# A graph attention kernel: one node span and one bank of sums for eight edge tiles instead of four

## The chip, the cores and the metric

The kernel runs on one core of a Trainium2 chip. The metric is device time in microseconds (us) of the whole program, as the median of several executions. A separate profiled execution of the same program gives the profile. Its engines are called PE (TensorE, matrix products), DVE (VectorE), ACT (ScalarE), POOL (GpSimd, which here issues the gathers) and SP (SyncE, which here issues the other transfers).

## The reference, cut to what matters

The input is a graph of 6250 nodes with 768 features each and 100,000 edges, sorted by their destination node. The layer normalises x, applies two graph attention layers (four heads, then one) and a small network of two dense layers, and adds the result to x:

```python
h = (x @ W).reshape(n, heads, -1)
e = leaky_relu(alpha_s[src] + alpha_d[dst], 0.2)      # one score per edge and head
e = exp(e - segment_max(e, dst)[dst])
alpha = e / (segment_sum(e, dst)[dst] + 1e-16)
out = segment_sum(h[src] * alpha, dst)                # sum over the edges of a node
```

Each node also has an edge to itself. What matters for this case is the last line: for every edge a row of h has to be fetched by its source, weighted, and added to the sum of its destination. As the edges are sorted, consecutive edges belong to the same or to neighbouring nodes; on average a node has 16 edges, so 128 edges cover about 8 nodes.

## The kernel before

**Tiles, groups and spans.** An edge tile is 128 edges, one per partition. There are 784 places for tiles (`NET`), in 196 groups of four (`NG`, `TPG`), or 98 units of two groups (`NU`). Nodes are in 49 tiles of 128 (`NT`). Group g covers 512 edges, some 32 nodes. The kernel pads 256 edges ahead of the first (`LEAD = 2 * P`), so that group g's edges lie around node 32g. It assumes that all their destinations lie in the span of 128 nodes from 32g-64 on. `hold` (L848) computes from `wbase` (L104) whether every edge's destination is in its group's span; if it is not, `general` (L959) recomputes everything in a slower way. As 256 padded edges are two tiles, the first group has two tiles of real edges (`FIRST`), the last has four; `tiles(g)` (L540) says which. There are 782 real tiles.

**Three stages.** A first stage normalises x and computes h for all nodes with TensorE (about the first 145 us), and writes it to a table in memory. Then `layer_edges` (L529) runs once for each attention layer.

**A group in `layer_edges`.** The loop over g (L706) does in order of each engine's queue:
- `gather(g + 8)` (L544): one indirect DMA per tile, issued by POOL, fetches 128 rows of the table into G. Two tiles share a buffer, of which there are 20.
- `pair(g, 0)` and, later in the group, `pair(g, 1)` (L613): for two tiles, ACT takes two exponentials of the source scores (L620, L622), DVE combines them with the factor of the destination (L625, and L635 or L628) to the weight w. In layer 1, DVE multiplies the gathered rows by w (`hw`, L637), and TensorE multiplies the one-hot matrix of destinations (`hot`, L583) by them; in layer 2, DVE makes a one-hot matrix that contains the weights (L632), and TensorE multiplies it by the gathered rows. Either way L648 adds the four tiles of a group into one PSUM bank, `o_ps[g]`. The row of a node in that sum is its number modulo 128, whatever the span. Three banks, under the tag "o", are in use in turn.
- The destination factors of each edge come from a matmul (`meet`, L593) of a mask with `pre.win`, whose entry is chosen by the group's span. The masks are made by DVE in layer 1 (`make_mask`, L561), stored to memory one unit of eight tiles at a time, and fetched again in layer 2 (`fetch_mask`, L523).
- `gather_up(g - 2)` (L659) at the end of a group takes up the bank of two groups earlier: `acc` is the running sum times `keep`, plus the bank (L673). `keep` (L117) is 0 in the one quarter (32 nodes) that enters the span anew, so old sums are dropped there, and 1 elsewhere. The quarter that has just left the span is then complete, and ACT copies it into `sum` (L681). After four quarters a node tile is complete, and its further work is put into the list `late`.
- `advance` (L685), twice a group, and four times in two groups near the end, lets each piece of work in `late` go one step on. In layer 1 (`Node1.steps`, L794) that is dividing, transposing, multiplying by W2 and writing the row block of layer 2's table (L817); in layer 2 (`Node2.steps`, L900) the two dense layers, adding x, and writing the output (L946).

**The ends.** The order of the last groups is written out by hand. Layer 2's first 11 tiles are gathered early (`first_rows`, L292, L300), by GpSimd behind layer 1's last gather: two of them need the table as far as node tile 45, nine as far as node tile 46; rows of later nodes are put in from on-chip copies (`first_whole`, L262). All other gathers of layer 2 need the whole table. For the last node tile, `whole` takes the sum of all groups but the last ahead of time, and only the last group's bank is added at the end.

**What sets the order.** Every engine works through its own queue in the order of the program; there is no planner. DVE's queue has, in one group: pair 0's three or four operations, the next one-hot matrix, the mask, pair 1's operations, and the addition of `gather_up`. Behind that addition stand the next group's pairs. ACT's copy of a quarter waits for the addition, and the next pair's exponentials are behind the copy.

Of the kernel before, what the change touches and what calls it, by code (L numbers as in the profile page):

```python
# [10 lines left out]
F32 = mybir.dt.float32  # L11
# [3 lines left out]
ALU = mybir.AluOpType  # L15
AX = mybir.AxisListType

P = 128
# [9 lines left out]
NT = -(-N // P)  # L28
NQ = 4 * NT
TPG = 4  # L30
NG = NQ
LEAD = 2 * P
EP = NG * TPG * P
NET = NG * TPG
FIRST = LEAD // P
# [18 lines left out]
def kernel(  # L54
# [33 lines left out]
    def bcast(src, n, off=0):  # L88
# [12 lines left out]
    nid = const.tile([P, NT], F32, name="nid")  # L101
    nc.gpsimd.iota(nid, pattern=[[P, NT]], base=0, channel_multiplier=1,
                   allow_small_or_imprecise_dtypes=True)
    wbase = const.tile([P, NG, TPG], F32, name="wbase")  # L104
    nc.gpsimd.iota(wbase, pattern=[[32, NG], [0, TPG]], base=-64, channel_multiplier=0,
                   allow_small_or_imprecise_dtypes=True)

    iota_ps = ps.tile([P, P], F32, name="iota_ps", bufs=1)
# [5 lines left out]
    ones_c = const.tile([P, 1], F32, name="ones_c")  # L114
    nc.vector.memset(ones_c, 1.0)

    keep = const.tile([P, 4], F32, name="keep")  # L117
    nc.vector.memset(keep, 1.0)
    for k in range(4):
        nc.vector.memset(keep[32 * k:32 * k + 32, k:k + 1], 0.0)  # L120

# [399 lines left out]
    def fetch_mask(u):  # L523

        if u < NU:
            mask[u] = maskp.tile([P, 8 * P], BF16, name="mask")
            nc.sync.dma_start(mask[u], mask_d[u * P:(u + 1) * P])

    def layer_edges(layer, H, node, pre, matched, pre_pool):  # L529

# [3 lines left out]
        with tc.tile_pool(name=f"eg{layer}", bufs=4) as eg, \  # L534
# [5 lines left out]
            def tiles(g):  # L540

                return range(max(TPG * g, FIRST) - TPG * g, min(TPG * g + TPG, LAST) - TPG * g)
# [18 lines left out]
            def make_mask(u):  # L561

                if not 0 <= u < NU:
                    return
                if layer == 2:
                    return fetch_mask(u + 1)
                a, b = (t * P for t in both(u))
                mask[u] = maskp.tile([P, 8 * P], BF16, name="mask")
                if u == 0:
                    nc.vector.memset(mask[u][:, :a], 0.0)  # L570
                at = u % 2 * 8 * P
                nc.vector.tensor_scalar(mask[u][:, a:b], drow[u // 2][:, at + a:at + b], pidx, None,  # L572
                                        ALU.is_equal)
                nc.sync.dma_start(mask_d[u * P:(u + 1) * P], mask[u])

            def make_hot(g):

# [15 lines left out]
            def meet(t):  # L593

                if t >= NT:
                    return
                e_ps[t] = ps.tile([P, 16, 6 * H], F32, name="e_ps", tag="e")
                for u, at, a, b in ranges(t):
                    m = mask.pop(u)
                    for k in range(a, b):  # L600
                        nc.tensor.matmul(e_ps[t][:, at + k, :3 * H], m[:, k * P:(k + 1) * P],  # L601
                                         pre.win[:, 2 * u + k // TPG + 1], start=True, stop=True)

            def join(t):
                if t >= NT:
# [7 lines left out]
            def pair(g, p):  # L613

                if 2 * p not in tiles(g):
                    return
                Gp = G.pop(TPG // 2 * g + p)
                sc = Gp[:, :, RW[1]:] if layer == 1 else Gp[:, :, HID:HID + 1]
                e1 = sm.tile([P, 2, H], F32, name="e1")
                nc.scalar.activation(e1, sc, AF.Exp)  # L620
                e2 = sm.tile([P, 2, H], F32, name="e2")
                nc.scalar.activation(e2, sc, AF.Exp, scale=SLOPE)  # L622
                at = TPG * (g % 4) + 2 * p
                rho, v, w = (e_ps[g // 4][:, at:at + 2, k * H:(k + 1) * H] for k in range(3, 6))
                nc.vector.tensor_mul(v, e2, rho)  # L625
                if layer == 2:
                    w = sm.tile([P, 2, H], F32, name="w")
                    nc.vector.tensor_max(w, v, e1)  # L628
                    hw = hwp.tile([P, 2, P], F32, name="hw")
                    for t in range(2):  # L630
                        k = TPG * g + 2 * p + t
                        nc.vector.tensor_scalar(hw[:, t], iota_ps, dcol[:, k:k + 1], w[:, t],  # L632
                                                ALU.is_equal, ALU.mult)
                else:
                    nc.vector.tensor_max(w, v, e1)  # L635
                    hw = hwp.tile([P, 2, H, C + 1], F32, name="hw")
                    nc.vector.tensor_mul(  # L637
                        hw, Gp[:, :, :RW[1]].rearrange("p t (h c) -> p t h c", h=H),
                        w.unsqueeze(3).to_broadcast([P, 2, H, C + 1]))
                if g not in o_ps:  # L640
                    o_ps[g] = ps.tile([P, RW[layer]], F32, name="o_ps", tag="o", bufs=3)
                for t in range(2):
                    k = 2 * p + t
                    if layer == 2:
                        l, r = hw[:, t], Gp[:, t]
                    else:
                        l, r = hot[g][:, k], hw[:, t].rearrange("p h c -> p (h c)")
                    nc.tensor.matmul(o_ps[g], l, r[:, :RW[layer]], start=(k == tiles(g)[0]),  # L648
                                     stop=(k == TPG - 1))

            def stay_warm(n):

# [3 lines left out]

            done, run, late, idle_ps = {}, {}, [], []

            def gather_up(g):  # L659

                if not 0 <= g < NG:
                    return
                last = g == NG - 1
                if last:

                    late.append(node.steps(NT - 1, None, run[0], o_ps.pop(g)))
                    return
                acc = sums.tile([P, RW[layer]], F32, name="acc")
                if g == 0:
                    nc.vector.tensor_copy(acc, o_ps.pop(g))  # L670
                else:
                    k = (g + 1) % 4
                    nc.vector.scalar_tensor_tensor(acc, run[0], keep[:, k:k + 1],  # L673
                                                   o_ps.pop(g), ALU.mult, ALU.add)
                run[0] = node.whole(NT - 1, acc) if g == NG - 2 else acc
                t, q = divmod(g - 2, 4)
                if 0 <= t < NT - 1:
                    if q == 0:
                        done[t] = sums.tile([P, RW[layer]], F32, name="sum", bufs=3)
                    r = slice(32 * q, 32 * q + 32)  # L680
                    nc.scalar.activation(done[t][r], acc[r], AF.Copy)  # L681
                    if q == 3:
                        late.append(node.steps(t, done.pop(t)))

            def advance(g):  # L685

# [19 lines left out]
            for g in range(NG):  # L706
# [4 lines left out]
                pair(g, 0)  # L711
                if g == NG - 1:
                    pair(g, 1)
                if g >= NG - 2:
                    gather_up(g - 1)
                advance(g)
                if g <= NG - 4:
                    make_hot(g + 1)
# [17 lines left out]
                advance(g)  # L736
                if j == 3:
                    join(t + 1)
                if g < NG - 2:
                    gather_up(g - 2)  # L740
                if g == NG - 3:
                    gather_up(g - 1)
                if NG - 3 <= g < NG - 1:
                    stay_warm(3)
                hot.pop(g, None)
                if layer == 1 and g == NG - 6:
                    first_sources(2)
            gather_up(NG - 1)
            advance(NG)
            stay_warm(4)  # L750
            if layer == 1:
# [501 lines left out]
```

## Time and profile before

| | |
|---|---|
| median of 3 executions | 2574.66 us (2572.14 to 2586.72) |
| the profiled execution's own time | 2137.04 us |
| its span, from first to last instruction | 2135.3 us |
| granted TensorE clock, mean over the span | 0.825 |
| PE busy | 1589.5 us (74%) |
| DVE busy | 1416.1 us (66%) |
| ACT busy | 593.1 us (28%) |
| POOL busy | 1600.6 us (75%) |

The profiled execution is 437.6 us faster than the median of the others. In lines of the profile, L12 is line 12 of the kernel, "out<-in" names what an instruction writes and reads, and "xcount" says how often it ran. Of a group of instructions the page gives the busy time and the mean of one in ns, and then, behind a second bar, how long the engine was idle just before them and what ended most of that idle time. "issue" stands where nothing that the profile shows was waited for. DMA-issuing instructions of SP and ACT are not counted as busy; the gathers of POOL are, for the time in which POOL prepares them.

### The profile page before, as it was taken

The page shows a single profiled execution, that of the slowest core. Times are in us where ns is not written, and L with a number is a line of the kernel's source. Part 1 is how long each engine was busy: PE and PEld are TensorE (multiplying, and loading weights), DVE is VectorE, ACT ScalarE, POOL GpSimd, SP SyncE. Part 2 cuts the span into 40 slices and gives each one's busy share as a digit, 9 for nine tenths or more (in the row PEclk, how much of TensorE's full clock was granted, in tenths as well). Part 3 has the DMA queues.
Part 4 walks back from the last instruction along what each step waited for, and adds up shares of the span by engine and source line. Part 5 has one row for each costly group of instructions (what it writes and reads, how often), then busy time and mean ns, then how long its engine had stood idle before and what let it go on. Part 6 is the DMA issues. An engine that isn't in the chain of part 4 may idle for free.

```text
span 2135.3 us, 26701 instructions
## 1 busy us (share of the span) xinstructions
PE 1589.5 (74%) x6763; PEld 1075.4 (50%) x6765; DVE 1416.1 (66%) x4359; ACT 593.1 (28%) x2601; POOL 1600.6 (75%) x1759
## 2 busy tenths in 40 slices
PE   8996777766767677666768677777767777777777
PEld 6874444444444444444445445545545545545544
DVE  7887777667677777677777655555555555555554
ACT  4651222222222222222222222222222222222222
POOL 6877777777777777777777777777777777777774
PEclk9998888677777767887779888888888888888888
DMA  9976666555555565565556455565555555565553
GB/s 356 363 232 206 169 172 176 165 169 163 167 170 163 170 170 162 169 168 158 166 143 211 130 180 166 169 181 166 169 181 166 169 181 166 169 181 167 168 171 114
DMA packets 157544, 383.26 MB, mean 179 GB/s; under 512 B 35543, under 2 KB 49966, under 8 KB 157382
## 3 DMA queue, kind: packets, MB, share of 16 engines
q0 software_dynamic: 75072, 209.10, 36.6%
q1 hardware_dynamic: 80940, 170.88, 23.1%
q10 hardware_dynamic: 1370, 1.48, 0.2%
q8 instruction: 58, 0.95, 0.2%
q14 instruction: 104, 0.85, 0.1%
HBM read 323.13 MB, written 58.19 MB: 179 GB/s over the span
## 4 chain that ended last, share of the span: by engine, by line
DMA 27%; PE 26%; DVE 26%; issue 9%; ACT 7%; POOL 5%; ACTq 0%; SPq 0%; POOLq 0%; DVEq 0%
DMA G<-table,src_i 26%; PE o_ps L648 11%; DVE hw L637 8%; PE y_ps L937 7%; POOL G L553 4%; PE h_ps L350 4%; DVE acc L673 3%; DVE e_ps L625 3%; ACT sum L681 3%; DVE e_ps L635 2%; ACT e L620 2%; DVE hw L632 2%; DVE mask L572 1%; ACT e L622 1%; PE y_ps L873 1%
## 5 line engine op out<-in xcount | busy, mean ns | idle before, releaser
L553 POOL DMA_INDIRECT G<-table,src_i x1545 | 1470.1, 952 | 472.3 <-issue 260.5
L648 PE MATMUL o_ps<-hw,hot 128*128 128x260 f32 x1564 | 596.7, 520 | 282.9 <-DVE hw L637 221.4
L648 PE MATMUL o_ps<-G,hw 128*128 128x258 f32 x1564 | 469.1, 432 | 229.8 <-DVE hw L632 229.1
L648 PEld LDWEIGHTS o_ps<-hw,hot 128*128 128x128 f32 x1564 | 352.9, 248 | 492.9 <-DVE hw L637 359.2
L625 DVE TENSOR_TENSOR e_ps<-e,e_ps 128x8 f32<-128x8 f32 (+1 forms) x782 | 128.4, 164 | 598.9 <-ACT e L622 597.5
L648 PEld LDWEIGHTS o_ps<-G,hw 128*128 128x128 f32 x1564 | 309.9, 212 | 348.3 <-DVE hw L632 290.5
L681 ACT ACTIVATE sum<-acc 32x260 f32<-32x260 f32 (+1 forms) x384 | 159.9, 416 | 776.9 <-DVE acc L673 775.3
L620 ACT ACTIVATE e<-G 128x8 f32<-128x8 f32 (+1 forms) x782 | 159.9, 204 | 617.8 <-DMA G<-table,src_i 576.4
L632 DVE TENSOR_SCALAR hw<-iota_ps,dcol,w 128x128 f32<-128x128 f32 x782 | 285.0, 406 | 14.4
L637 DVE TENSOR_TENSOR hw<-G,e_ps 128x520 f32<-128x520 f32 x391 | 271.9, 695 | 15.2 <-DVE e_ps L635 2.0
L937 PE MATMUL y_ps<-wm,mT 128*128 128x384 f32 x392 | 206.5, 664 | 0.7 <-ACT mT L926 0.7
L673 DVE SCALAR_TENSOR_TENSOR acc<-acc,keep,o_ps 128x260 f32<-128x260 f32 (+1 forms) x388 | 184.5, 476 | 0.1
L622 ACT ACTIVATE e<-G 128x8 f32<-128x8 f32 (+1 forms) x782 | 148.9, 190 | 0.2
L350 PE MATMUL h_ps<-w,r 128*128 128x256 f32 x588 | 133.0, 380 | 4.4 <-ACT r L341 4.4
L583 DVE TENSOR_TENSOR hot<-iota_ps,dcol 128x512 f32<-128x512 f32 (+1 forms) x196 | 133.5, 682 | 0.0
L937 PEld LDWEIGHTS y_ps<-wm,mT 128*128 128x128 f32 x392 | 88.3, 249 | 66.9 <-issue 40.9
L350 PEld LDWEIGHTS h_ps<-w,r 128*128 128x128 f32 x588 | 108.0, 190 | 21.8 <-ACT r L341 5.7
L635 DVE TENSOR_TENSOR e_ps<-e_ps,e 128x8 f32<-128x8 f32 x391 | 68.1, 174 | 13.4
L365 POOL TENSOR_TENSOR ha<-kept,a1b 128x512 f32<-128x512 f32 x45 | 53.2, 1183 | 23.9 <-ACT kept L356 23.8
L628 DVE TENSOR_TENSOR w<-e_ps,e 128x2 f32<-128x2 f32 x391 | 62.2, 159 | 13.3
L601 PEld LDWEIGHTS <-mask 128*128 128x128 bf16 x1564 | 57.7, 101 | 11.4 <-issue 1.7
L767 ACT ACTIVATE rT<-tp,bT 128x128 f32<-128x128 f32 x196 | 59.4, 352 | 6.6 <-PE tp L761 6.4
(405 smaller groups left out, 1137.7 us busy)
## 6 DMA issues: line engine op xcount, KB each, us to landing
xt<-in_x SPq DMA_DIRECT2D x96, 384.0 KB, 4.8
drow<-dmod_d SPq DMA_DIRECT2D x49, 512.0 KB, 6.4
mask_d<-mask SPq DMA_DIRECT2D x98, 256.0 KB, 2.2
mask<-mask_d SPq DMA_DIRECT2D x98, 256.0 KB, 5.9
G<-table,src_i POOLq DMA_INDIRECT x1545, 2.9
xTt<-in_xT SPq DMA_DIRECT2D x49, 384.0 KB, 5.9
out<-y SPq DMA_DIRECT2D x48, 384.0 KB
table<-kept SPq DMA_DIRECT2D x49, 132.0 KB, 3.7
```

The costliest lines, as they stand in the source:

```text
L350: nc.tensor.matmul(h_ps, r[:, k], w1[:, k], start=(k == 0), stop=(k == KI - 1))
L553: nc.gpsimd.indirect_dma_start(out=G[k // 2][:, k % 2], out_offset=None, in_=table[layer], in_offset=bass.IndirectOffsetOnAxis(ap=src_i[:, ...
L583: nc.vector.tensor_tensor(hot[g][:, T[0]:T[0] + n], iota_ps.unsqueeze(1).to_broadcast([P, n, P]), dcol[:, k:k + n].unsqueeze(2).to_broadca ...
L620: nc.scalar.activation(e1, sc, AF.Exp)
L622: nc.scalar.activation(e2, sc, AF.Exp, scale=SLOPE)
L625: nc.vector.tensor_mul(v, e2, rho)
L632: nc.vector.tensor_scalar(hw[:, t], iota_ps, dcol[:, k:k + 1], w[:, t], ALU.is_equal, ALU.mult)
L637: nc.vector.tensor_mul(hw, Gp[:, :, :RW[1]].rearrange("p t (h c) -> p t h c", h=H), w.unsqueeze(3).to_broadcast([P, 2, H, C + 1]))
L648: nc.tensor.matmul(o_ps[g], l, r[:, :RW[layer]], start=(k == tiles(g)[0]), stop=(k == TPG - 1))
L673: nc.vector.scalar_tensor_tensor(acc, run[0], keep[:, k:k + 1], o_ps.pop(g), ALU.mult, ALU.add)
L681: nc.scalar.activation(done[t][r], acc[r], AF.Copy)
L937: nc.tensor.matmul(y_ps, mT[:, j], wm2[:, j, s * half:(s + 1) * half], start=False, stop=(j == KH - 1))
```

## The change

One span of 128 nodes now serves a unit of two groups. The padding ahead of the first edge goes (`LEAD = 0`), so unit u covers 1024 edges around nodes 64u to 64u+63, and its span is the 128 nodes from 64u-32 on. Group 0 has four real tiles then, and the last group two; there are still 782. All eight tiles of a unit use the same entry of `pre.win`, and their products are added up in one bank, `o_ps[u]`. `gather_up(u)` takes it up at the end of group 2u+5 (other groups near the end), and copies two finished quarters at once instead of one; `keep` is 0 in the two quarters that enter the span. In the last but one unit a quarter that is no longer part of the last node tile is cleared. Masks are stored and fetched only as wide as they have real tiles. `wbase`, from which the guard is computed, follows the new spans.

```diff
-LEAD = 2 * P
+LEAD = 0
...
-    wbase = const.tile([P, NG, TPG], F32, name="wbase")
-    nc.gpsimd.iota(wbase, pattern=[[32, NG], [0, TPG]], base=-64, channel_multiplier=0,
+    wbase = const.tile([P, NU, 2 * TPG], F32, name="wbase")
+    nc.gpsimd.iota(wbase, pattern=[[64, NU], [0, 2 * TPG]], base=-32, channel_multiplier=0,
...
-    keep = const.tile([P, 4], F32, name="keep")
+    keep = const.tile([P, 2], F32, name="keep")
     nc.vector.memset(keep, 1.0)
-    for k in range(4):
-        nc.vector.memset(keep[32 * k:32 * k + 32, k:k + 1], 0.0)
+    for k, q in ((0, 1), (0, 2), (1, 3), (1, 0)):
+        nc.vector.memset(keep[32 * q:32 * q + 32, k:k + 1], 0.0)
...
         if u < NU:
+            b = (min(8 * u + 8, LAST) - 8 * u) * P
             mask[u] = maskp.tile([P, 8 * P], BF16, name="mask")
-            nc.sync.dma_start(mask[u], mask_d[u * P:(u + 1) * P])
+            nc.sync.dma_start(mask[u][:, :b], mask_d[u * P:(u + 1) * P, :b])
...
-                if u == 0:
-                    nc.vector.memset(mask[u][:, :a], 0.0)
...
-                nc.sync.dma_start(mask_d[u * P:(u + 1) * P], mask[u])
+                nc.sync.dma_start(mask_d[u * P:(u + 1) * P, a:b], mask[u][:, a:b])
...
-                                         pre.win[:, 2 * u + k // TPG + 1], start=True, stop=True)
+                                         pre.win[:, 2 * u + 2], start=True, stop=True)
...
-                if g not in o_ps:
-                    o_ps[g] = ps.tile([P, RW[layer]], F32, name="o_ps", tag="o", bufs=3)
+                u = g // 2
+                if u not in o_ps:
+                    o_ps[u] = ps.tile([P, RW[layer]], F32, name="o_ps", tag="o", bufs=3)
...
-                    nc.tensor.matmul(o_ps[g], l, r[:, :RW[layer]], start=(k == tiles(g)[0]),
-                                     stop=(k == TPG - 1))
+                    nc.tensor.matmul(o_ps[u], l, r[:, :RW[layer]], start=(g % 2 == 0 and k == 0),
+                                     stop=(g % 2 == 1 and k == tiles(g)[-1]))
...
-            def gather_up(g):
-
-                if not 0 <= g < NG:
-                    return
-                last = g == NG - 1
-                if last:
-
-                    late.append(node.steps(NT - 1, None, run[0], o_ps.pop(g)))
+            def gather_up(u):
+
+                if u == NU - 1:
+
+                    late.append(node.steps(NT - 1, None, run[0], o_ps.pop(u)))
                     return
                 acc = sums.tile([P, RW[layer]], F32, name="acc")
-                if g == 0:
-                    nc.vector.tensor_copy(acc, o_ps.pop(g))
+                if u == 0:
+                    nc.vector.tensor_copy(acc, o_ps.pop(u))
                 else:
-                    k = (g + 1) % 4
-                    nc.vector.scalar_tensor_tensor(acc, run[0], keep[:, k:k + 1],
-                                                   o_ps.pop(g), ALU.mult, ALU.add)
-                run[0] = node.whole(NT - 1, acc) if g == NG - 2 else acc
-                t, q = divmod(g - 2, 4)
-                if 0 <= t < NT - 1:
+                    nc.vector.scalar_tensor_tensor(acc, run[0], keep[:, u % 2:u % 2 + 1],
+                                                   o_ps.pop(u), ALU.mult, ALU.add)
+                for Q in (2 * u - 1, 2 * u):
+                    t, q = divmod(Q, 4)
+                    if not 0 <= t < NT - 1:
+                        continue
...
+                if u == NU - 2:
+                    nc.vector.memset(acc[96:], 0.0)
+                    run[0] = node.whole(NT - 1, acc)
+                else:
+                    run[0] = acc
...
-                if g >= NG - 2:
-                    gather_up(g - 1)
+                if g == NG - 2:
+                    gather_up(NU - 2)
...
-                if g < NG - 2:
-                    gather_up(g - 2)
-                if g == NG - 3:
-                    gather_up(g - 1)
+                if g % 2 and 5 <= g < NG - 6:
+                    gather_up((g - 5) // 2)
+                elif g in (NG - 6, NG - 5, NG - 3):
+                    gather_up({NG - 6: NU - 5, NG - 5: NU - 4, NG - 3: NU - 3}[g])
...
-            gather_up(NG - 1)
+            gather_up(NU - 1)
```

## The prediction, made before the result was known

> **What bounds the kernel now.** I read the page's busy shares first, then equal stretches of both edge passes, then GpSimd's instructions one by one where the passes begin and end, and last the chain of waits inside layer 1. The span of the profiled execution is 2135.3 us, its own time 2137.04 us.
>
> ```profile
> span 2135.3 us, 26701 instructions
> ...
> PE 1589.5 (74%) x6763; PEld 1075.4 (50%) x6765; DVE 1416.1 (66%) x4359; ACT 593.1 (28%) x2601; POOL 1600.6 (75%) x1759
> ```
>
> VectorE (DVE) and GpSimd (POOL) are both well short of full by this count. The costliest groups show what the rest of POOL's time is.
>
> ```profile
> L553 POOL DMA_INDIRECT G<-table,src_i x1545 | 1470.1, 952 | 472.3 <-issue 260.5
> L681 ACT ACTIVATE sum<-acc 32x260 f32<-32x260 f32 (+1 forms) x384 | 159.9, 416 | 776.9 <-DVE acc L673 775.3
> L673 DVE SCALAR_TENSOR_TENSOR acc<-acc,keep,o_ps 128x260 f32<-128x260 f32 (+1 forms) x388 | 184.5, 476 | 0.1
> ```
>
> A gather (L553) keeps POOL for 952 ns, with about 0.30 us before the next: 1545 of them leave 472.3 us of gaps, 0.306 each. The stretches of 400 us (columns PE, PEld, DVE, ACT, POOL) show whether those gaps ever grow:
>
> ```profile
> 200.00:600.00 400.00, 282.55 (x1121) 183.73 (x1121) 297.65 (x828) 97.17 (x495) 303.33 (x318) 0.78 0.60 169
> 600.00:1000.00 400.00, 278.30 (x1077) 181.81 (x1076) 286.28 (x796) 97.47 (x476) 303.12 (x319) 0.76 0.59 166
> 1200.00:1600.00 400.00, 301.18 (x1354) 200.76 (x1354) 229.07 (x825) 108.87 (x499) 302.63 (x320) 0.84 0.57 172
> 1600.00:2000.00 400.00, 305.33 (x1362) 203.98 (x1362) 228.70 (x822) 109.75 (x500) 302.53 (x321) 0.84 0.58 172
> ```
>
> They do not. POOL does 318 to 321 gathers in every stretch, 1.25 us each, although layer 2 asks a fifth less of VectorE and more of TensorE than layer 1. So the gathers set the pace: four tiles, one group, take 5.0 us. GpSimd's order of time where layer 1 hands over to layer 2 shows the only stall:
>
> ```profile
> 1130.08 0.95 POOL L553 DMA_INDIRECT G<-table,src_i  x1 [0.30 <-issue]
> 1131.33 0.95 POOL L300 DMA_INDIRECT G<-table,first_i  x1 [0.30 <-DVE e_ps L625]
> ...
> 1133.82 0.95 POOL L300 DMA_INDIRECT G<-table,first_i  x1 [0.30 <-ACT e L620]
> ...
> 1146.78 0.94 POOL L553 DMA_INDIRECT G<-table,src_i  x1 [1.89 <-DVE G L275]
> ```
>
> Layer 2's early gathers follow layer 1's last without a pause; the one idle of 1.89 us, 1.59 above the usual, comes when the gathers need the whole table. In all, 1564 gathers run from 144.6 to 2111.6 us: 1967 of 2135.3, with 144.6 ahead and 23.7 behind. The compute beside them has slack. This is the chain inside layer 1, at a place where it is catching up:
>
> ```profile
> 601.78 0.43 ACT sum L681
> 602.23 0.21 ACT e L620
> ...
> 605.63 0.41 DVE acc L673
> 606.06 0.42 ACT sum L681
> ```
>
> From one sum to the next is one group: 4.28 us through ScalarE and VectorE, 0.7 under the gathers' 5.0.
>
> **Profiled time and runs.** The median, 2574.66, is 1.2048 times the profiled execution's 2137.04, and the profile does not say why. [...] I take all engines to be slowed alike in the timed runs, so that POOL bounds them too and ratios carry over.
>
> [...]
>
> **The change, part by part** (times of the profiled execution).
>
> *VectorE's take-up.* Before, each layer has 194 additions at L673 and one copy; after, one copy and 96 additions. So 196 fewer in all: 196 x 0.476 = 93.3 us of VectorE. Worth 0, because gathers hide it; were that cover gone it is at most 93.3 us, 4.4%. It widens slack: a group without take-up skips 0.41 (addition) + 0.43 (copy) + 0.32 (the exponentials queued behind the copy) = 1.16 us of the 4.28 chain and comes to 3.1; one with it has a second copy and comes to 4.7. Mean 3.9.
>
> *ScalarE's copies of finished quarters.* 192 a layer before and after; two come together, so the next pair's exponentials wait 0.42 us longer in every second group. Under the same cover: 0.
>
> *Small VectorE work.* Two new memsets on 32 partitions x 260. Not shown; those shown take 0.06 (128x1) and 0.17 us (128x128): 0.06 to 0.5 each, I take 0.2, ahead of layer-end work that waits for later matmuls anyhow. The first mask's memset (0.17) goes. 0, at most 1.
>
> *Bank.* The 3128 matmuls of L648 stay; one bank collects eight. Unit u+3's first matmul needs the bank of u, whose addition stands in VectorE's queue at the end of group 2u+5, ahead of the weights (L637, L632) that this matmul waits for anyway. 0. Exposed each time it would be 96 x 0.476 x 2 = 91 us of TensorE, against 95 to 122 us idle in each 400: hidden still.
>
> *Padding.* Layers still have 1564 tiles together, but group 0 gets four and group 195 two, instead of two and four. Relative to the gathers, each group comes two tiles, 2.5 us, later. At the start this costs nothing: GpSimd first needs an old buffer at its 41st gather (20 buffers of two tiles), 144.6 + 40 x 1.25 = 194.6 us, and the first buffer comes free near 178.5. Masks: 98 writes and 98 reads on SyncE as before, the last of each two tiles shorter. 0.
>
> *Node steps.* Tile t is finished at the end of group 4t+9, not 4t+7; for the last three tiles the ends are written out and stay at their groups. Layer 1: the early gathers at 1131.33 need the row block of tile 45. Its first step, 1096.8 now, moves two groups and 2.5 us to 1109.3; since calls double from group 192, the eight further calls to its store take three groups (15 us), not four (20.7 from 1096.8 to the store's issue at 1117.5): 1124.3, plus issue and the 3.7 us of such a store: 1128.4. Slack 2.9 us. Tile 46 (needed 1133.82) is stored 2.5 us later, near 1130.6, landing at 1134.3: 0.5 late, inside the 1.59 that the queue stands still for the full table. That table depends on the last pair, whose gather is no later. Handover: 0, from -1 to +2. In layer 2 the load of x's last tile on SyncE now waits for tile 44's last addition; behind it are only outputs and the last masks, needed some 20 us on: 0.
>
> *End.* After the last gather 23.7 us remain. One pair's four matmul passes less at the very end: -1.1 (eight took 2.17). The steps of tile 47 start 2.5 us later against the gathers, partly hidden because TensorE is behind them by about 3 us already, and one 1.56 us output product of tile 45 moves into this stretch. I take +0.5, from -1.1 to +4.
>
> Sum: 2135.3 + 0 + 0 + 0.5 = 2135.8 us span, 2137.5 own time; times 1.2048, 2575 us.
>
> **Rivals.** *The likeliest, no change:* 2575, its own range 2564 to 2586 with the scatter of the runs shown (2572 to 2587). Chance 0.82.
>
> *VectorE and ScalarE bound the timed runs, and it gets faster.* For it: L681 waits 775 us for L673, and the chain runs through both wherever compute catches up. Against: the profile shows 0.7 us of slack a group. The 437 us extra, put on 392 groups, are 1.1 us each, so this chain would have to be slowed from 4.28 to 6.1 us, by 1.43, with POOL at its pace. If so, layer 1 gains up to 0.38/4.28 of 6.1 us = 0.54 x 195 = 106 us: 2470, half of that more likely, 2520. Chance 0.09.
>
> *The handover stalls, and it gets slower.* GpSimd's queue is in order: if tile 45's store lands after 1131.3, every later gather is late by the excess. It decides from 2.9 us beyond my figure; 13 us beyond, it adds 10 us, or 12 in a timed run: 2587. For it: two groups later by the written order. Against: the doubled calls. Chance 0.08.
>
> *The change falls to the general path.* The guard now asks that every edge's node lie within 128 of 64u-32. From the reference's seeded edges, offsets run from 28 to 114 (44 to 97 before): it holds. Chance 0.01; no row of the profile prices that path, and I count it as slower.
>
> **How the numbers follow.** 0.5% (13 us) is about what a measurement of this kernel can tell from no change. Faster 0.09, same 0.82, slower 0.09. The likeliest's range holds about 0.78 of all; reaching a little into both rivals gives 2555 to 2590.
>
> **What would show it.** Right: 318 to 321 gathers per 400 us in both layers; L673 x192 near 0.476; VectorE's total near 1323 us with a like span; the gap before the early gathers still 0.30. Wrong: gathers slower or faster than 1.25 us; idle above 2 us ahead of L300; more than 28 us behind the last gather; or timed runs that move while the profiled one doesn't, which would mean that the profiled execution has another bound than the runs.

## The result, and the profile after

The kernel after takes 2580.97 us (median of 20 runs, 2572.73 to 2588.72) and the kernel before, run beside it, 2576.76 us (20 runs): a ratio of 1.0018, interval 1.0004 to 1.0032. I had forecast 2575 us and no change. The number came out; a step on which it rests did not.

The same kernel before takes about 2137 us in some batches of runs (its profiled execution, and the first batch of experiments below) and 2577 to 2622 us in others (the timed runs above, and the later batches); since the profile after is from an execution of 2581 us, the two profiles show two conditions, called short and long below, as well as two kernels.

The head of the page of the kernel after, and its groups of the gathers, of ScalarE's copies and of the additions (busy time, mean ns of one, then idle time ahead of them and what ended it):

```profile
span 2579.5 us, 26528 instructions
...
PE 1611.5 (62%) x6764; PEld 1134.1 (44%) x6765; DVE 1328.8 (52%) x4164; ACT 543.7 (21%) x2601; POOL 1600.1 (62%) x1759
```

```profile
L554 POOL DMA_INDIRECT G<-table,src_i x1545 | 1469.8, 951 | 849.3 <-issue 622.3 <-ACT mT L928 134.8 <-ACT e L621 32.3
L678 ACT ACTIVATE sum<-acc 32x260 f32<-32x260 f32 (+1 forms) x384 | 159.9, 416 | 1067.0 <-DVE acc L669 793.7 <-remote 68.5 <-DVE hw L636 63.8
L669 DVE SCALAR_TENSOR_TENSOR acc<-acc,keep,o_ps 128x260 f32<-128x260 f32 (+1 forms) x192 | 91.1, 475 | 0.0
```

The change is there: 192 additions for 388, VectorE's total down from 1416.1 to 1328.8 us (I had 1323). But look at the durations beside those of before: a gather 951 ns against 952, an addition 475 against 476, a copy 416 both times. The execution is 444 us longer, and none of these instructions is slower. TensorE alone is busy longer, 1611.5 us against 1589.5 for as many matmuls, at a lower granted clock (0.753 against 0.825). Nearly all of the rest is idle time, for GpSimd 849.3 us ahead of the gathers against 472.3. The same stretches of 400 us as shown of before (PE, PEld, DVE, ACT, POOL, granted clock, DMA share, GB/s):

```profile
200.00:600.00 400.00, 212.45 (x868) 142.15 (x869) 220.99 (x614) 64.98 (x373) 243.79 (x256) 0.71 0.48 137
600.00:1000.00 400.00, 224.55 (x898) 151.48 (x896) 222.77 (x623) 69.68 (x396) 250.22 (x262) 0.70 0.47 137
1200.00:1600.00 400.00, 236.88 (x976) 160.72 (x975) 198.56 (x636) 70.71 (x376) 228.05 (x240) 0.71 0.42 125
1600.00:2000.00 400.00, 263.63 (x1141) 186.69 (x1139) 174.18 (x654) 85.19 (x425) 260.02 (x276) 0.77 0.49 147
```

256 to 276 gathers where there were 318 to 321 (240 in the stretch with the handover), and VectorE and ScalarE down in step. GpSimd's order of time at the handover says who waits for whom:

```profile
1347.90 0.95 POOL L554 DMA_INDIRECT G<-table,src_i  x1 [0.30 <-issue]
1383.05 0.94 POOL L300 DMA_INDIRECT G<-table,first_i  x1 [34.21 <-ACT sum L678]
...
1389.23 0.94 POOL L300 DMA_INDIRECT G<-table,first_i  x1 [3.98 <-DVE e_ps L634]
...
1401.60 0.94 POOL L554 DMA_INDIRECT G<-table,src_i  x1 [1.24 <-issue]
```

The first early gather of layer 2 stands 34.21 us, where it was issued without a pause before. GpSimd had run ahead and filled every buffer. Counted over layer 1 from the starts in the trace, the gathers are 36 tiles ahead of the pair whose rows VectorE multiplies (median; at most 38 of the 40 that the buffers hold), against 4 in the 2137-us execution of before. In the trace of before a gather lands 2.9 us after its issue in the median, and 36 tiles take GpSimd 45 us at 1.25 each: in this execution rows are there in time and GpSimd waits for buffers, so gathers do not set its pace. Behind the last gather 50.8 us remain (23.7 before), the same backlog being worked off.

Most of the time is lost in long waits. Between 200 and 2450 us VectorE waits 35 times for more than 7 us, 350 us in all; the profile of before has no such wait there. One of them, in order of time (start, duration, engine; in brackets the idle time before and its releaser):

```profile
610.00 0.69 DVE L636 TENSOR_TENSOR hw<-G,e_ps 128x520 f32<-128x520 f32 x1
...
611.17 0.38 PE L648 MATMUL o_ps<-hw,hot 128*128 128x260 f32 x1 [0.49 <-DVE hw L636]
...
613.29 0.38 PE L648 MATMUL o_ps<-hw,hot 128*128 128x260 f32 x1 [1.74 <-issue]
...
616.08 0.59 PE L648 MATMUL o_ps<-hw,hot 128*128 128x260 f32 x1 [2.41 <-issue]
...
618.87 0.59 PE L648 MATMUL o_ps<-hw,hot 128*128 128x260 f32 x1 [2.21 <-issue]
...
621.78 0.69 DVE L582 TENSOR_TENSOR hot<-iota_ps,dcol 128x512 f32<-128x512 f32 x1 [11.09 <-remote]
...
624.62 0.94 POOL L554 DMA_INDIRECT G<-table,src_i  x1 [6.28 <-issue]
```

Four matmuls, whose inputs VectorE had written by 610.69 us, come 2.1 to 2.8 us apart; VectorE waits 11.09 us, by the program for one of the four buffers of `hot` that these matmuls read, and GpSimd in the end, by the program too, for a buffer of G. One warning on such rows: this trace holds 12,826 records of signals where the one of before holds 42,927, so "issue" and "remote" here mean only that no releaser was recorded.

### The profile page after: what moved, and what is told of

Same layout as the page of the kernel before. It is cut to its first block, busy times and chain, and to the rows that moved or that the text cites. A ratio compares the mean times of both kernels' runs of the same rounds, so it can differ in the third digit from the quotient of the medians.

```text
span 2579.5 us, 26528 instructions
## 1 busy us (share of the span) xinstructions
PE 1611.5 (62%) x6764; PEld 1134.1 (44%) x6765; DVE 1328.8 (52%) x4164; ACT 543.7 (21%) x2601; POOL 1600.1 (62%) x1759
## 3 DMA queue, kind: packets, MB, share of 16 engines
q0 software_dynamic: 75072, 209.10, 29.9%
## 4 chain that ended last, share of the span: by engine, by line
DVE 31%; another core or an unknown queue 28%; issue 19%; PE 16%; ACT 5%; DMA 1%; POOL 0%; ACTq 0%; DVEq 0%; POOLq 0%
DVE hw L636 8%; PE o_ps L648 7%; DVE hw L631 6%; PE h_ps L350 4%; DVE e_ps L624 3%; PE y_ps L939 2%; ACT sum L678 2%; DVE acc L669 2%; DVE e_ps L634 2%; DVE mask L571 2%; DVE w L627 2%; PE tp L923 1%; DVE hot L582 1%; DVE y L942 1%
## 5 line engine op out<-in xcount | busy, mean ns | idle before, releaser
L554 POOL DMA_INDIRECT G<-table,src_i x1545 | 1469.8, 951 | 849.3 <-issue 622.3
L648 PE MATMUL o_ps<-hw,hot 128*128 128x260 f32 x1564 | 567.4, 499 | 436.0 <-issue 231.5
L648 PE MATMUL o_ps<-G,hw 128*128 128x258 f32 x1564 | 485.7, 460 | 55.2 <-issue 36.8
L648 PEld LDWEIGHTS o_ps<-G,hw 128*128 128x128 f32 x1564 | 352.6, 233 | 156.9 <-issue 52.8
L582 DVE TENSOR_TENSOR hot<-iota_ps,dcol 128x512 f32<-128x512 f32 x196 | 133.6, 682 | 242.0 <-remote 227.0
L600 PE MATMUL e_ps<-win,mask 128*128 128x12 bf16 (+1 forms) x1564 | 74.7, 170 | 178.8 <-issue 168.3
L939 PE MATMUL y_ps<-wm,mT 128*128 128x384 f32 x392 | 160.1, 532 | 13.1 <-issue 12.3
L942 DVE TENSOR_TENSOR y<-y_ps,xt 128x384 f32<-128x384 f32 (+1 forms) x98 | 54.0, 552 | 221.3 <-remote 194.8
L923 PE MATMUL tp<-rT,wm 128*128 128x128 f32 x392 | 71.0, 338 | 130.0 <-issue 87.5
L923 PEld LDWEIGHTS tp<-rT,wm 128*128 128x128 f32 x392 | 62.1, 237 | 145.5 <-issue 96.5
L814 PE MATMUL h_ps<-w,rT 128*128 128x258 f32 x196 | 76.8, 533 | 62.1 <-ACT rT L769 62.1
```

Of the source, the lines that this page charges most:

```text
L554: nc.gpsimd.indirect_dma_start(out=G[k // 2][:, k % 2], out_offset=None, in_=table[layer], in_offset=bass.IndirectOffsetOnAxis(ap=src_i[:, ...
L582: nc.vector.tensor_tensor(hot[g][:, T[0]:T[0] + n], iota_ps.unsqueeze(1).to_broadcast([P, n, P]), dcol[:, k:k + n].unsqueeze(2).to_broadca ...
L648: nc.tensor.matmul(o_ps[u], l, r[:, :RW[layer]], start=(g % 2 == 0 and k == 0), stop=(g % 2 == 1 and k == tiles(g)[-1]))
L923: nc.tensor.matmul(m_ps[:, j], wm1[:, k, j * P:(j + 1) * P], rT[:, k], start=(k == 0), stop=(k == KH - 1))
L939: nc.tensor.matmul(y_ps, mT[:, j], wm2[:, j, s * half:(s + 1) * half], start=False, stop=(j == KH - 1))
```

## The experiments

Three theories were tried. G: gathers at 1.25 us set the pace. T: in the long executions the time is what TensorE needs to issue. S: signals come late there, because of the many landings. Kernels of one batch share their runs of before. The first three batches ran on one chip, which so shows both conditions.

**More gathers** (first batch; before 2137.15 us, and once more by itself 2136.74: the short condition, which says nothing of the long one).

> The kernel before, unchanged, profiled once more. Theory G (the prediction's: the gathers' pace of 1.25 us bounds every execution, and the timed runs are slower by 1.2 on all engines alike): either 2137 us with 320 gathers in 400 us as in the first profile, or near 2575 us with each gather at 1.14 us of POOL and each addition at 0.57 us, 1.2 times the first profile's 0.952 and 0.476. Theory T (TensorE comes late in the usual execution, and the gathers wait for it): near 2575 us with gathers still at 0.95 us and additions at 0.476 us, but only 255 to 275 gathers in 400 us, and idle time of TensorE that the profile explains by nothing.

```diff
+                tc.tile_pool(name=f"xg{layer}", bufs=2) as xg, \
...
+                if g % 2 and g > 3:
+                    again = xg.tile([P, TW[layer]], F32, name="again")
+                    nc.gpsimd.indirect_dma_start(
+                        out=again, out_offset=None, in_=table[layer],
+                        in_offset=bass.IndirectOffsetOnAxis(ap=src_i[:, k:k + 1], axis=0))
```

> The changed kernel, with every gather of the odd groups from the fifth on issued a second time into a scratch buffer that nobody reads: some 770 gathers more, on POOL alone. Theory G: 770 x 1.25 = 963 us more at the first profile's pace, 1155 more in a timed run: near 3730 us. Theory T: POOL uses 1964 of 2575 us for 1564 gathers (1.25 each); with 2334 it needs 2918 us and becomes the bound, so some 145 + 2918 + 25 = 3090 us, 500 more, and TensorE's delays hide behind it.

The edit stands behind the loop over tiles, so it added 192 gathers, not the 770 of the expectation: theory G's figure becomes 192 x 1.25 = 240 us. Measured: 2383.2 us, 246 more (ratio 1.1147, 1.1128 to 1.1165). The stretch from 200 us and the group of the added gathers:

```profile
200.00:600.00 400.00, 256.70 (x976) 172.00 (x975) 248.87 (x691) 87.84 (x433) 303.70 (x317) 0.73 0.56 160
...
L560 POOL DMA_INDIRECT again<-table,src_i x192 | 181.9, 948 | 58.5 <-issue 29.3 <-DVE e_ps L640 9.7 <-PE o_ps L654 8.8
```

317 gathers, as before, of which a part now are useless: each added one costs its 0.948 + 0.30 us in full, 240 of the 246 us. The kernel after by itself was not run in the short condition, so all comparisons there are with before. In the short condition G is right.

**No meeting of scores** (first batch).

```diff
+                nc.vector.memset(e_ps[t][:, :, :3 * H], 0.25)
...
-                    m = mask.pop(u)
-                    for k in range(a, b):
-                        nc.tensor.matmul(e_ps[t][:, at + k, :3 * H], m[:, k * P:(k + 1) * P],
-                                         pre.win[:, 2 * u + 2], start=True, stop=True)
+                    mask.pop(u)
```

> The changed kernel without the matmuls that hand each edge the factor of its destination (1564 short matmuls and as many weight loads on TensorE, a third of TensorE's instructions in the edge passes by number, under a tenth by busy time); a constant written by VectorE stands in their place, so the weights are not those of the reference. Theory G: no change, 2575 us within 13. Theory T: the unexplained idle time of TensorE ahead of these matmuls was 352 us in the changed kernel's profile; if their number is what makes TensorE late, the time falls by 200 to 440 us, to between 2140 and 2380.

2142.18 us, 5.0 above before, ratio 1.0027 (1.002 to 1.0034): a quarter of TensorE's matmuls is worth nothing here, and T is not touched: the trace of before in this condition has none of the runs of matmuls or weight loads 0.7 or 1.4 us apart that the profile after has 50 to 70 times. The kernel holds the change, so it also shows its handover undisturbed:

```profile
1132.30 0.95 POOL L300 DMA_INDIRECT G<-table,first_i  x1 [0.30 <-issue]
...
1136.63 0.94 POOL L300 DMA_INDIRECT G<-table,first_i  x1 [2.13 <-DVE e_ps L632]
...
1148.62 0.94 POOL L554 DMA_INDIRECT G<-table,src_i  x1 [0.58 <-DVE G L275]
```

The third early gather, the first that needs tile 46, waits 2.13 us; the wait for the full table shrinks from 1.89 to 0.58. The step from early to full table comes at 1148.62 against 1146.78 and 1147.46 in two executions of before: 1.2 to 1.8 us later. Of this, 0.7 to 0.9 us arose after the first early gather (16.32 us from there to the full table, against 15.45 and 15.67); the rest was there before the handover.

**The additions given back, twice.** A second addition into a tile that nobody reads, first from two tensors in SBUF (first batch), then from the bank in PSUM as the real one (second batch; before 2618.28 us).

```diff
+                if u:
+                    twice = sums.tile([P, RW[layer]], F32, name="twice", bufs=2)
+                    nc.vector.scalar_tensor_tensor(twice, run[0], keep[:, u % 2:u % 2 + 1], acc,
+                                                   ALU.mult, ALU.add)
```

> The changed kernel, with each of VectorE's 192 additions of a bank done a second time into a scratch buffer, so that VectorE has as much to do as in the kernel before: 192 x 0.476 = 91 us. Theory G and theory T: no change, 2581 us within 13, since VectorE has slack behind either. The rival of a bound on VectorE: 91 us more or, at the timed runs' pace, 110.

2154.67 us, ratio 1.0079 (1.0062 to 1.0096): 17.5 us, where neither view had it. The gathers' row shows the price: 960 ns each for 952, times 1545 is 12 us. The other 5.5 us are near the 5.0 of the kernel without score matmuls, which holds the change too.

```profile
L554 POOL DMA_INDIRECT G<-table,src_i x1545 | 1483.4, 960 | 470.6 <-issue 261.7 <-ACT e L621 47.5 <-PE o_ps L648 46.9
```

In the other traces of this batch with the real additions alone, 388 or 192 of them, the gathers take 951 to 954 ns. So this was not a clean way of giving VectorE its work back; why these additions lengthen the gathers this run alone does not show. The second form replaces `acc` in the added line by `o_ps[u]`, ahead of the real addition:

> The kernel after, with each of its 192 additions done once more into a tile that nobody reads; the second one reads the bank of sums in PSUM and the running sum in SBUF, as the real one does. VectorE gets its 91 us of additions back and everything else stays as in the kernel after. Theory G (the additions are hidden by the gathers and don't disturb GpSimd): within 3 us of the kernel after, a gather at 951 to 953 ns. Rival: it was not the two SBUF inputs but any addition that slows the gathers, as seen with the earlier doubled additions: again +12 to +17 us over the kernel after, a gather near 960 ns.

2593.53 us against 2593.05 for the kernel after in the same batch; VectorE's busy time is up by 75 us (1404.2 against 1329.0). In the long condition too, then, these additions are worth nothing. The gathers' mean is 957 ns here, 951 to 953 in the three traces of the kernel after. The kernel before has 388 additions that read one tensor from SBUF and one from PSUM, as the 384 here do, and its gathers take 951 and 952 ns in two traces of the short condition. So the 957 may be scatter, or belong to the long condition; no run tells which.

**The kernel after, again** (second batch, and third with before at 2622.02 us).

> The kernel after as it stands, beside the kernel before on one chip. Gathers set the pace (theory G): a ratio of 1.000 to 1.003, with 317 to 321 gathers in each 400 us of both layers where the profiled execution is near 2137 us; what is lost, 2 to 6 us, is lost at the handover between the layers (idle above 1.9 us ahead of an early gather of layer 2, 1.59 us of it before) and behind the last gather (more than 23.7 us). VectorE and ScalarE set the pace (rival): a ratio below 0.99.

> The kernel after as it stands, once more, beside the two kernels that follow. If the kernel before takes about 2137 us here (no late TensorE), theory G: 2138 to 2143 us, ratio 1.0005 to 1.003, the loss at the handover and behind the last gather. If it takes about 2577 us or more (TensorE issuing its instructions 0.7 or 1.4 us apart for some 10 us once in a node tile, theory T): a ratio between 0.99 and 1.002, since it came out at both ends.

Ratios of 0.9902 (0.9888 to 0.9917) and 0.9924 (0.9899 to 0.9949): 25 and 21 us faster, where the result's comparison had 4 us slower. The kernel after lies at 2581, 2593 and 2601 us in the three, before at 2577, 2618 and 2622. Against before in these batches it is 0.8 to 1% faster, in the result's own it is not; why before differs by 1.6 to 1.8% between them I did not find.

**Half of the gathers** (second batch). In both kernels the second tile of a pair uses the rows of the first.

```diff
-                    if k < FIRST + len(THERE[layer]):
+                    if k < FIRST + len(THERE[layer]) or k % 2:
...
-                Gp = G.pop(TPG // 2 * g + p)
+                Gp = G.pop(TPG // 2 * g + p)[:, 0:1].to_broadcast([P, 2, TW[layer]])
```

> The kernel before with the rows of every second tile left out: of each two tiles the second uses the rows gathered for the first, so the sums are of the wrong rows, but every other engine does the same work. GpSimd then needs 2.5 us for a group and no longer sets the pace. Theory G: layer 1 falls from 5.0 us a group to the chain's 4.28 (minus 141 us), layer 2 from 5.0 to about 4 (TensorE busy 3.8 a group; minus 196 us): 1800 us, from 1740 to 1900. If something else than the gathers set the pace: within 30 us of the kernel before.

> The kernel after with the rows of every second tile left out, as in the other kernel of this name. With the gathers' cover gone, the take-up counts: my working put the chain of layer 1 at 3.9 us a group after against 4.28 before (75 us less over 196 groups), and layer 2 is bound by TensorE in both; so 1725 us, 50 to 93 us below the halved kernel before (ratio of the two 0.95 to 0.975). Rival: TensorE or the latency from one engine to the next bounds both, and the take-up is off the path even then: the two within 15 us of each other.

1847.0 and 1707.89 us: the change gains 139 us once the gathers' cover is off (ratio of the two 0.925), more than the 50 to 93 expected. Stretches from 200 and from 1200 us, before halved, then after halved:

```profile
200.00:600.00 400.00, 285.36 (x1197) 183.79 (x1195) 317.21 (x887) 95.59 (x520) 178.91 (x179) 0.85 0.44 127
...
1200.00:1600.00 400.00, 352.09 (x1831) 239.74 (x1829) 300.65 (x1100) 135.09 (x675) 203.12 (x215) 1.00 0.51 160
```

```profile
200.00:600.00 400.00, 287.82 (x1292) 201.81 (x1291) 324.80 (x913) 96.69 (x559) 191.09 (x194) 0.85 0.47 137
...
1200.00:1600.00 400.00, 382.26 (x2058) 272.43 (x2058) 310.56 (x1183) 148.25 (x756) 229.30 (x243) 1.00 0.58 180
```

Layer 1 goes from 179 to 194 gathers in the first stretch, layer 2 from 215 to 243. By the gathers' starts, layer 1 (first gather to first early gather of layer 2) takes 909.0 and 851.2 us: 58 us, 0.30 a group, near my 0.38. What follows takes 790.9 and 709.0: 82 us, where I had put nothing, and TensorE's row shows it waiting less (382.26 us busy of 400, not 352.09). Which part of the change gives layer 2 this was not tried.

The second finding is the size: with half the gathers the same compute takes 1708 us in the very batch in which the full kernel takes 2593. All 1564 gathers at GpSimd's pace, with what lies ahead and behind, are the 2135 us of before's span in the short condition, so some 450 of the 2593 us are explained by neither alone. The halved traces lack records of signals as well: they hold 20,979 and 18,468, against 42,546 to 45,566 in the traces of the first batch. Half of the gathers accounts for a part only, as the 192 added ones brought some 2,900 records. So the loss of records goes with the batch and not with a long execution.

**Earlier take-up, and the missing matmuls in the long condition** (third batch).

```diff
-                if g % 2 and 5 <= g < NG - 6:
-                    gather_up((g - 5) // 2)
-                elif g in (NG - 6, NG - 5, NG - 3):
-                    gather_up({NG - 6: NU - 5, NG - 5: NU - 4, NG - 3: NU - 3}[g])
+                if g % 2 and 3 <= g < NG - 2:
+                    gather_up((g - 3) // 2)
```

> The kernel after with the sums taken up two groups earlier (at the end of group 2u+3, as soon as the second group of the bank is done), so that tile 45's and 46's rows are stored two groups earlier for the handover; nothing else changes. If the kernel before takes about 2137 us here, theory G with a late handover: 2 to 4 us below the kernel after, back at the 1.9 us idle ahead of layer 2's full table and less than 2 us ahead of any early gather. Rival, the loss is at the end of layer 2 alone: within 1 us of the kernel after. If it takes 2577 us or more: within 10 us of the kernel after.

2588.63 us, 12 below the kernel after, where within 10 was expected (2583 to 2600 against 2594 to 2610): the ranges overlap, so nothing is settled. Its waits ahead of the first and the third early gather add up to 36.6 us, against 37.9 in the kernel after of the same batch.

> The kernel after without the matmuls that bring the destination's scores to the edges (a constant in their place; 1564 matmuls and 1564 weight loads fewer on TensorE, a quarter of its instructions, and the weights of the sums are then wrong). If the kernel before takes about 2137 us here: 2140 to 2144 us, as gathers set the pace. If it takes 2577 us or more, theory T (the time is what TensorE needs to issue its instructions): 200 to 440 us less than the kernel after. Rival (all engines or the gathers are slower there): within 30 us of the kernel after.

2548.47 us, ratio 0.9721 (0.9681 to 0.976): 52 us below the kernel after, a fair miss for both. T falls, since of the runs of matmuls or weight loads 0.7 or 1.4 us apart (by how strictly one counts, 50 to 70 places in the profile after, 320 to 430 us) none is left here, and the time is still 2548 us.

This is also, word for word, the kernel that took 2142.18 us in the first batch, so it shows the two conditions without any difference of kernels. First short, then long:

```profile
PE 1558.7 (73%) x5200; PEld 1033.5 (48%) x5201; DVE 1360.0 (64%) x4262; ACT 594.4 (28%) x2601; POOL 1603.4 (75%) x1759
...
L554 POOL DMA_INDIRECT G<-table,src_i x1545 | 1472.7, 953 | 471.0 <-issue 261.7
```

```profile
PE 1603.1 (63%) x5199; PEld 1090.7 (43%) x5201; DVE 1342.3 (53%) x4262; ACT 545.9 (21%) x2601; POOL 1604.7 (63%) x1759
...
L554 POOL DMA_INDIRECT G<-table,src_i x1545 | 1473.9, 954 | 811.0 <-issue 584.8
```

A gather takes 953 and 954 ns, an addition 476 and 475. TensorE is busy 44 us longer, at a granted clock of 0.749 against 0.830, which is about a ninth of the 406 us between the two; whether the lower clock is a cause or comes of the waiting, no run tells. The rest is waiting.

The lateness shows even where no other engine is waited for. Three rows of VectorE in the long execution:

```profile
641.37 0.16 DVE L622 TENSOR_TENSOR e_ps<-e,e_ps 128x8 f32<-128x8 f32 x1
...
644.01 0.17 DVE L632 TENSOR_TENSOR e_ps<-e_ps,e 128x8 f32<-128x8 f32 x1 [2.47 <-remote]
...
645.41 0.70 DVE L634 TENSOR_TENSOR hw<-G,e_ps 128x520 f32<-128x520 f32 x1 [1.22 <-DVE e_ps L632]
```

The maximum (L632) takes what the product (L622) has just written on the same engine, and by the program the only signal that it waits for is VectorE's own (for 28 of the waits ahead of it, 30.0 us in sum, the trace names that product; for the one above it names none); its other input, ScalarE's first exponential, was made ahead of the second, which the product already had. It follows after 0.034 us in the median of all kernels; here after 2.47. Delays over 0.5 us in this one pair of instructions (391 in all): 58 in this kernel, 107 us in sum, up to 3.9; 10 to 15 in the three traces of the kernel after; none in the executions of the short condition, none in the halved kernels. So an engine's signal comes late even to itself, or the instruction that waits for it does; the trace doesn't tell these two apart.

**Half of the gathers, all of the transfers** (fourth batch, on another chip; before 2620.81 us).

```diff
+                tc.tile_pool(name=f"xg{layer}", bufs=8) as xg, \
...
+                    if k % 2:
+                        plain = xg.tile([P, TW[layer]], F32, name="plain")
+                        nc.sync.dma_start(plain, x[k % 32 * P:(k % 32 + 1) * P, :TW[layer]])
+                        continue
```

> The halved kernel after, in which the second of each two tiles uses the rows of the first (so its sums are of the wrong rows), with a plain transfer issued by SyncE in place of each gather that was left out: 128 rows of 1 KB of x into a tile that nobody reads. The DMA engines then land as many transfers as in the kernel after, but GpSimd issues half of them. Theory S (where the kernel before takes about 2577 us or more, it is the signals of the landings, or their bursts, that make every engine's waits end late): near 2500 us, from 2350 to 2600, and waits of VectorE on its own last instruction of 0.5 to 3.9 us, which are 0.034 us in the halved kernel. Theory P (it is GpSimd's own gathers, 1.25 us each or made dearer, that set the pace there too): 1710 to 1780 us as in the halved kernel (1708), with no such waits. If the kernel before takes about 2137 us: 1710 to 1780 us by both.

1716.38 us, 8 above the halved kernel, with none of those delays: the 391 maxima have 13.3 us of idle ahead of them in all, 0.034 each. The edit leaves the DMA engines about as many bytes to move as in the kernel after, and they move more of them in the stretch from 200 us (208 GB/s, 137 in the kernel after):

```profile
200.00:600.00 400.00, 287.19 (x1297) 201.02 (x1296) 324.51 (x912) 97.61 (x565) 190.54 (x194) 0.86 0.70 208
```

So S falls in the form in which I put it: with as many landings and bytes, none of the delays came. Theory P's number came out, 1710 to 1780, but P as worded falls by the 36 tiles of rows that the long execution keeps in hand. What is shown is narrower: the delays came with the full set of GpSimd's gathers and not with half of it, which takes away waits for them on the other engines as well. Which of these two counts, and what sets the condition off, stay open.

## Why the prediction was right, and where not

**What bounds the kernel.** Right for the profiled execution that I read: in that condition 192 added gathers cost 246 us, a quarter of the matmuls nothing. Wrong for the timed runs. The step that failed is "I take all engines to be slowed alike in the timed runs, so that POOL bounds them too and ratios carry over". It was my estimate from the one ratio, 1.2048, and no trace of an execution as long as the runs stood behind it; the profile after has a gather at 951 ns and an addition at 475, neither of them slower than the 952 and 476 of before. A ratio of two times was no evidence of which instructions are longer. In the long condition gathers are 36 tiles ahead, and waits end late (VectorE's for its own last result up to 3.1 us late in the profile after, where the median is 0.034). Of my signs of being wrong, the profile after shows fewer gathers in 400 us (240 to 276), idle above 2 us ahead of L300 (34.21) and more than 28 us behind the last gather (50.8). They mean what the last sign was to mean: the profiled execution had another bound than the runs. That the ratio came out near 1 in the timed runs all the same is luck, as far as my argument goes. In the two later batches it is 0.990 and 0.992, and the medians of 2593 and 2601 us lie above my range.

**VectorE's take-up worth 0.** It came out, on two grounds. In the short condition the gathers hide it, as I argued: without 196 of the additions and without the score matmuls the time is 2142.18 us, not below the 2137.15 of before. In the long condition it is not hidden by gathers, and giving VectorE 75 us back still moves nothing (2593.5 against 2593.1). So the 25 us by which the kernel after is faster in that batch are not VectorE's additions either; what they are stays open. The compute itself is 139 us quicker when uncovered; what is left over the halved kernel is 2618 - 1847 = 771 us for before and 2593 - 1708 = 885 for after. So of the 139 us only 25 are left in the full kernels of that batch, and 114 go into longer waiting. That is arithmetic over one batch; no run shows which waits they are.

**"Were that cover gone it is at most 93.3 us".** Mis-sized: 139. I had summed busy time; a hop from engine to engine in every second group goes with it, which is my explanation and no run's, and layer 2, for which I had no gain, brought 82 of it.

**ScalarE's copies, masks, padding, bank.** Copies 384 in all, as said. The memsets on 32 partitions were estimated at 0.2 us and took 0.27 each. No row shows a wait for the bank; the first gather starts at 147.2 us (144.6 and 146.4 in two executions of before): nothing.

**Handover, 0 from -1 to +2.** In the short condition the full table is taken up 1.2 to 1.8 us later, 0.7 to 0.9 of it from the handover itself, and tile 46 is the late one, as worked out, 1.8 us rather than 0.5 (0.85 in the second execution of before, whose third early gather waits 1.15 with the usual 0.30 in it). In the long condition it is another matter, as GpSimd stands for 34.2 + 4.0 us. The two halved kernels, in which GpSimd waits as well, show what before has in its place: 29.9 + 9.1 us of idle ahead of the same two gathers, against 36.7 + 4.0 after: 1.6 us more.

**End, +0.5 from -1.1 to +4.** 25.0 us behind the last gather without the score matmuls, against 22.8 and 23.7: +1.3 to +2.2. The step to the full table and the end together make 2.5 to 4 of the 5.0 us by which that kernel is slower than before; my sum had 0.5 for both. The 50.8 us of the profile after are above my bound of 28 and belong to its backlog: both halved kernels have 54 to 55.

**The rivals.** The one in which VectorE and ScalarE bound the timed runs was right that GpSimd does not bound them, and wrong in its price: 2470 to 2520 us, measured 2581. The later batches, 0.8 to 1% faster, lean its way; the result's comparison does not, and VectorE's 75 us speak against VectorE as the bound. A stall at the handover and the general path did not come.

## What to carry to other kernels

When the timed runs and the profiled execution of one kernel differ by a fifth, don't scale: ask for the profile of an execution that is as long as the runs, and see whether durations or idle times have grown, and how far ahead the producer is. Cover is best measured by taking it away: halving the gathers gave in two runs what the change is worth without them (139 us, not 93). And a useless copy of an instruction is best given the same kinds of operands as the original: with two inputs in SBUF the copies came with gathers of 960 ns, where they take 951 to 954 with the real additions alone.

## What the runs showed that I had not expected

- One kernel takes 2137 or some 2577 to 2622 us on this hardware. In the kernel that was traced in both conditions (2142 and 2548 us) the durations of gathers and additions are equal, and TensorE is busy 44 us longer. The rest is waits, down to an engine's wait for its own last result (0.034 us in the median, up to 3.9 us).
- The lateness goes with GpSimd's gathers: half of them, 1708 us; half of them and as many plain transfers, 1716; all of them, 2593.
- A trace of a long execution holds less than a third of the signal records of a short one (12,826 against 42,927), which spoils the names of releasers exactly where they are wanted. The halved kernels in the later batches lose records too (20,979 and 18,468 left) and are not late (no delay over 0.5 us between those two instructions), so the loss alone does not make the lateness. Whether the recording has a part in it wasn't tried.
- With 192 additions more that have two SBUF inputs, the 1545 gathers took 960 ns in the mean instead of 952.
